# Query-key products of a sparse attention layer: summed over features on TensorE by accumulated transposes, with biases added by transposes

## The chip, the cores and the metric

The kernel runs on one core of a Trainium2 chip. The metric is the device time of the whole kernel in microseconds (us). A core has TensorE (PE, matrix products; its weight loads are listed as PEld), VectorE (DVE), ScalarE (ACT), GpSimd (POOL), and SyncE (SP), which here only starts transfers. The engines run side by side, each works through its own instructions in order, and they wait for each other by semaphores. Products of PE land in PSUM, eight banks of 128 partitions by 512 fp32 numbers.

## What is computed

Two graph layers over 8 batches of 2048 nodes with 256 features. A node has few neighbours (the adjacency is sparse and symmetric, with the diagonal). Layer 0 is attention with 4 heads of 64 features, whose softmax runs over chunks of 256 nodes, with absent edges at a score of -10:

```python
q = (x @ Wq.T + bq).reshape(B, N, H, Dh).transpose(0, 2, 1, 3)
k = (x @ Wk.T + bk)...
v = (x @ Wv.T + bv)...
scores = jnp.einsum('bhnd,bhjcd->bhnjc', q, kc) / jnp.sqrt(Dh)
scores = jnp.clip(scores, -10.0, 10.0)
scores = jnp.where(mask == 0, -10.0, scores)
attn = jax.nn.softmax(scores, axis=-1)          # over the 256 nodes of a chunk
ctx = jnp.einsum('bhnjc,bhjcd->bhnd', attn, vc)
out = ctx @ Wo.T + bo + x
out = layernorm(out) * gamma + beta
x = _layernorm(x + out)
# ... layer 1: a second graph attention, whose scores are s_src + s_dst of
# Wh = x @ W, then softmax over neighbours, sum of Wh, elu
x = _layernorm(x + layer1)
```

## The kernel before

The kernel builds a list of neighbours for each node (24 places), sorts the nodes by their number of neighbours, and cuts them into 16 tiles of 128 nodes. Tile t has room for `CAPS[t]` neighbours. Two batches make a group, so there are 4 groups of layer 0, 64 iterations, each for one group and tile. For layer 1 two groups are taken together, 32 iterations. A table of keys and values (`kv_d`), made by `tables`, lies in HBM; GpSimd gathers from it one row of 4 KB per node and neighbour slot, two slots to a unit, into a ring of 12 units.

```python
G = 2; UNIT = 2; RING = 12       # batches per group, neighbours per unit, units
CAPS = (24, 14, 13, 12, 11, 11, 10, 10, 9, 9, 8, 8, 7, 7, 6, 5)
# GF = 512: features of a group; GH = 8: heads of a group; KC = 2; D = 64; NCH = 8
```

A PSUM bank is taken by tag; the tags `tk` (2 banks), `tf` (1), `acc` (3) and `mf` (2) make up the eight banks:

```python
    def bank(tag, bufs=2):

        return ps.tile([P, 512], F32, tag=tag, name=tag, bufs=bufs)
    def transposed(t, tag, bufs):

        pt = bank(tag, bufs).rearrange("p (c r) -> p c r", r=P)
        for c in range(G * KC):
            nc.tensor.transpose(pt[:, c, :], t[:, c * P:(c + 1) * P], ident)
        return pt
```

The tables of one tile: transposes of x, keys and values of each batch, queries of both. The bias is added by a product of a row of ones with the bias row:

```python
    def tables(g, t):
        if t == 0:
            vsum[g] = small.tile([P, G * KC, NT], F32, tag="xs", name="xs")
        qx = xts.pop((g, t))
        pt = transposed(qx[:, GF:], "tk", 2)
        xT = work.tile([P, G * KC, P], F32, tag="xT", name="xT")
        for c in range(G * KC):
            nc.scalar.activation(xT[:, c, :], pt[:, c, :], AF.Copy, accum_out=vsum[g][:, c, t:t + 1])
        kvs = work.tile([P, 2 * GF], F32, tag="kvs", name="kvs", bufs=1)
        view = kvs.rearrange("p (m b f) -> p b m f", m=2, b=G)
        for b in range(G):
            pm = bank("tk")
            for kc in range(KC):
                nc.tensor.matmul(pm, xT[:, b * KC + kc, :], wkv[:, kc, :], start=(kc == 0), stop=False, skip_group_check=True)
            nc.tensor.matmul(pm[:, 0:F], ones1, bk_r, start=False, stop=True, skip_group_check=True)
            nc.scalar.copy(view[:, b], pm.rearrange("p (m f) -> p m f", m=2))
        nc.sync.dma_start(kv_d[g][t * P:(t + 1) * P, :], kvs)
        q = bank("tk")
        for b in range(G):
            qb = q[:, b * F:(b + 1) * F]
            for kc in range(KC):
                nc.tensor.matmul(qb, xT[:, b * KC + kc, :], wq[:, kc, :], start=(b == 0 and kc == 0), stop=False,
                                 skip_group_check=True)
            nc.tensor.matmul(qb, ones1, bq_r, start=False, stop=True, skip_group_check=True)
        nc.scalar.copy(qx[:, 0:GF], q)
        nc.sync.dma_start(qx_d[g][t * P:(t + 1) * P, :], qx)
    # ... (sums of v per chunk after the last tile)
```

The weighting of gathered rows and their sum, by transposes that accumulate in PSUM:

```python
    def weighted(part, al, s0, n):

        e = part.shape[2] // D
        pv = part.rearrange("p s (e d) -> p s e d", d=D)
        av = al[:, :, s0:s0 + n].rearrange("p e s -> p s e").unsqueeze(3).to_broadcast([P, n, e, D])
        nc.vector.tensor_tensor(pv, pv, av, op=ALU.mult)

    def summed(acc, part, first, last):

        n = part.shape[1]
        for k in range(n):
            for c in range(G * KC):
                nc.tensor.matmul(acc[:, c, :], part[:, k, c * P:(c + 1) * P], ident, is_transpose=True,
                                 start=first and k == 0 and c == 0, stop=last and k == n - 1, skip_group_check=True)
```

Layer 0. `scores0` multiplies the gathered keys by the query in place, and reduces over the 64 features of each head; both run on VectorE:

```python
    def fetch0(g, t):
        qx = work.tile([P, 2 * GF], F32, tag="qx", name="qx", bufs=3)
        nc.gpsimd.indirect_dma_start(out=qx, out_offset=None, in_=qx_d[g],
                                     in_offset=bass.IndirectOffsetOnAxis(ap=node[:, t:t + 1], axis=0))
        got0[g, t] = qx, gather(2 * GF, kv_d[g], t)

    def scores0(g, t):
        S = CAPS[t]
        qx, units = got0[g, t][:2]
        sc = small.tile([P, GH, S], F32, tag="sc", name="sc")
        for u, s0, n in units:
            part = u[:, :, 0:GF]
            nc.vector.tensor_tensor(part, part, qx[:, 0:GF].unsqueeze(1).to_broadcast([P, n, GF]), op=ALU.mult)
            nc.vector.tensor_reduce(sc[:, :, s0:s0 + n].rearrange("p e s -> p s e"),
                                    part.rearrange("p s (e d) -> p s e d", d=D), axis=AX.X, op=ALU.add)
        st0[g, t] = sc

    def softmax0(g, t):
        S = CAPS[t]
        sc = st0.pop((g, t))
        nc.vector.tensor_scalar(sc, sc, -10.0, 10.0, op0=ALU.max, op1=ALU.min)
        e = small.tile([P, GH, S], F32, tag="e", name="e", bufs=1)
        nc.scalar.activation(e, sc, AF.Exp)
        nc.vector.scalar_tensor_tensor(e, e, -EMIN, valid[:, t, 0:S].unsqueeze(1).to_broadcast([P, GH, S]),
                                       op0=ALU.add, op1=ALU.mult)
        # ... sums of e by chunk into z, its reciprocal, the weights al
        pz = bank("tf", 1)[0:H * NCH, 0:G * P].rearrange("p (b r) -> p b r", b=G)
        for b in range(G):
            nc.tensor.transpose(pz[:, b, :], z[:, b * H:(b + 1) * H, :].rearrange("p h c -> p (h c)"), ident)
        zT = small.tile([H * NCH, G, P], F32, tag="zT", name="zT")
        nc.scalar.copy(zT, pz)
        st0[g, t] = al, zT

    def context0(g, t):
        S = CAPS[t]
        al, zT = st0.pop((g, t))
        units = got0[g, t][1]
        acc = bank("acc", 3).rearrange("p (c r) -> p c r", r=P)
        for b in range(G):
            for kc in range(KC):
                nc.tensor.matmul(acc[:, b * KC + kc, :], vsum[g][:, b, kc * P:(kc + 1) * P], zT[:, b, :],
                                 start=(b == 0 and kc == 0), stop=False, skip_group_check=True)
        for u, s0, n in units:
            weighted(u[:, :, GF:2 * GF], al, s0, n)
            summed(acc, u[:, :, GF:2 * GF], False, s0 + n == S)
        cT = work.tile([P, G * KC, P], F32, tag="cT", name="cT", bufs=1)
        nc.scalar.copy(cT, acc)
        st0[g, t] = cT
    def finish0(g, t):
        cT = st0.pop((g, t))
        qx, _, xb = got0.pop((g, t))
        po = bank("mf").rearrange("p (b f) -> p b f", b=G)
        for b in range(G):
            for kc in range(KC):
                nc.tensor.matmul(po[:, b, :], cT[:, b * KC + kc, :], wo[:, kc, :], start=(b == 0 and kc == 0),
                                 stop=False, skip_group_check=True)
            nc.tensor.matmul(po[:, b, :], ones1, bo_r, start=False, stop=True, skip_group_check=True)
        o = work.tile([P, G, F], F32, tag="o", name="o")
        nc.vector.tensor_tensor(o, po, qx[:, GF:].rearrange("p (b f) -> p b f", b=G), op=ALU.add)
        # ... moments, layer norms (VectorE, with Ln and Exp on ScalarE)
        normalized(o, o, G)
        nc.sync.dma_start(x1_d[g // 2][t * P:(t + 1) * P, g % 2, :].rearrange("p (b f) -> p b f", b=G), o)

        pt = transposed(o.rearrange("p b f -> p (b f)"), "tf", 1)
        xT = work.tile([P, G * KC, P], F32, tag="x1T", name="x1T", bufs=1)
        nc.scalar.copy(xT, pt)
        wh = work.tile([P, WW], F32, tag="whs", name="whs")
        for b in range(G):
            pw = bank("mf")
            for kc in range(KC):
                nc.tensor.matmul(pw[:, 0:F + 2 * H], xT[:, b * KC + kc, :], wa[:, kc, :], start=(kc == 0), stop=(kc == KC - 1))
            nc.scalar.copy(wh[:, b * F:(b + 1) * F], pw[:, 0:F])
            nc.scalar.copy(sd[g // 2 % 2][:, t, g % 2, b * H:(b + 1) * H], pw[:, F:F + H])
            nc.scalar.copy(wh[:, GF + b * H:GF + (b + 1) * H], pw[:, F + H:F + 2 * H])
        # ... scatter of wh by GpSimd
```

Layer 1's `context1` uses two `acc` banks per iteration (one per group of the pair), and its `finish1` turns the sums back through `mf`, one bank for each of the two:

```python
        for k, hT in enumerate(hTs):
            ph = bank("mf")
            for c in range(G * KC):
                nc.tensor.transpose(ph[:, c * P:(c + 1) * P], hT[:, c, :], ident)

            nc.scalar.activation(y[:, k], ph, AF.Exp)
            nc.vector.scalar_tensor_tensor(xr[:, k], ph, 0.0, xr[:, k], op0=ALU.max, op1=ALU.add)
            # ...
```

The sequence: groups 0 and 1 of layer 0 first, then groups 2 and 3 with the first half of layer 1 between them, then the rest of layer 1. Instructions are ordered for each engine when the program is built, so that those of neighbouring steps are interleaved:

```python
    seq = [(0, i) for i in range(2 * NT)]
    for t in range(NT):
        seq += [(0, 2 * NT + 2 * t), (0, 2 * NT + 2 * t + 1), (1, t)]
    seq += [(1, NT + t) for t in range(NT)]
# ...
    for k, (layer, i) in enumerate(seq):
        g, t = i // NT, i % NT
        if layer == 0:
            shift0(g, t)
        scatters()
        # ... fetch of the next step
        if layer == 0:
            scores0(g, t)
            if i:
                finish0((i - 1) // NT, (i - 1) % NT)
            if g + 1 < NG:
                if i + NT + 1 < NG * NT:
                    load_x((i + NT + 1) // NT, (i + 1) % NT)
                tables(g + 1, t)
            if k + 1 < len(seq) and seq[k + 1] == (0, (g + 1) * NT):
                fetch[0](seq[k + 1][1])
            softmax0(g, t)
            context0(g, t)
        else:
            softmax1(g, t)
            if i:
                finish1((i - 1) // NT, (i - 1) % NT)
            context1(g, t)
```

## Time and profile before

| | before |
|---|---|
| time, median of 3 runs | 3197.0 us (3189.07 to 3202.07) |
| span of the profiled execution | 3192.1 us |
| instructions | 31721 |
| TensorE clock granted, mean | 0.771 |
| HBM read and written | 604.31 MB and 117.96 MB |

The span is the time from the first to the last instruction. A group of the profile is named by its line in the kernel, the engine and the operation, with the tile written and the tiles read; behind the bar stand its busy time, the mean duration of one instruction in ns, and the idle time of the engine just before, with what ended it. An fp32 product of the program stands as two records on PE and a transpose as one: the 128 products with `bk_r` are 256 records, the 256 transposes of `qxs` 256. Records of PE overlap each other, so that a duration is longer than the time from one start to the next. The line numbers are those of the kernel before.

### The profile page before, as it was taken

How to read it: one execution, taken by the hardware profiler on the slowest of the kernel's cores; microseconds unless marked ns; L12 is line 12 of the kernel's file. 1: busy time of each engine (PE TensorE's matmuls, PEld its weight loads, DVE VectorE, ACT ScalarE, POOL GpSimd, SP SyncE). 2: the span in 40 equal slices, each digit the busy share in tenths (PEclk: the TensorE clock that was granted, in tenths of full speed). 3: DMA queues.
4: the chain of work that ended last, by engine and by line, in shares of the span. 5: the costliest groups of instructions: out<-in, count | busy, mean ns of one | idle time of the engine just before them, and what ended most of it. 6: DMA issues, size and time to landing. Idle time of an engine off the chain costs nothing. (4 is left out here: it accounts for less than half of the span.)

```text
span 3192.1 us, 31721 instructions
## 1 busy us (share of the span) xinstructions
PE 1991.3 (62%) x9554; PEld 1373.5 (43%) x9554; DVE 2512.5 (79%) x4912; ACT 695.1 (22%) x2140; POOL 1746.2 (55%) x1364
## 2 busy tenths in 40 slices
PE   7988955599988886554455555453554554346553
PEld 3444534355555554333344444342433443235452
DVE  5925789886688888777989988889999887368785
ACT  3632211133322222111011111111111212112222
POOL 0053656534276445436667666557776543488873
PEclk8999977789997888666777776676776667677876
DMA  5645765566477756426657666636676653367771
GB/s 194 231 143 215 287 230 189 199 212 218 171 264 260 257 203 227 151 94 203 228 189 264 223 229 215 208 114 240 220 243 227 230 180 110 131 213 274 269 250 66
DMA packets 219466, 660.18 MB, mean 207 GB/s; under 512 B 43688, under 2 KB 61867, under 8 KB 217239
## 3 DMA queue, kind: packets, MB, share of 16 engines
q0 software_dynamic: 162688, 521.98, 48.2%
q1 hardware_dynamic: 52880, 126.11, 10.7%
q10 hardware_dynamic: 3718, 9.97, 0.9%
q8 instruction: 79, 1.29, 0.2%
q14 instruction: 101, 0.82, 0.1%
HBM read 604.31 MB, written 117.96 MB: 226 GB/s over the span
## 5 line engine op out<-in xcount | busy, mean ns | idle before, releaser
L385 POOL DMA_INDIRECT u<-kv_d,idx x656 | 812.8, 1239 | 323.4 <-issue 143.0
L404 PE MATMUL acc<-ident,u 128*128 128x128 f32 x5248 | 692.0, 293 | 247.5 <-DVE u L397 236.2
L404 PEld LDWEIGHTS acc<-ident,u 128*128 128x128 f32 x5248 | 640.1, 152 | 297.5 <-DVE u L397 271.7
L426 DVE TENSOR_TENSOR u<-u,qx 128x1024 f32<-128x1024 f32 (+1 forms) x344 | 401.6, 1177 | 164.8 <-DMA u<-kv_d,idx 131.9
L274 PE MATMUL tf<-ident,o 128*128 128x128 f32 x256 | 68.9, 410 | 712.4 <-ACT o L377 712.3
L385 POOL DMA_INDIRECT u<-wh_d,idx x328 | 420.4, 1282 | 129.0 <-issue 70.7
L515 POOL DMA_INDIRECT wh_d<-whs,node x64 | 144.5, 2258 | 593.4 <-ACT zT L458 542.6
L427 DVE TENSOR_REDUCE sc<-u 128x16 f32<-128x1024 f32 (+1 forms) x344 | 393.2, 1158 | 0.8
L397 DVE TENSOR_TENSOR u<-u,e 128x1024 f32<-128x1024 f32 (+1 forms) x344 | 387.6, 1164 | 0.2
L397 DVE TENSOR_TENSOR u<-u,al 128x1024 f32<-128x1024 f32 (+1 forms) x344 | 386.0, 1175 | 0.6
L274 PEld LDWEIGHTS tf<-ident,o 128*128 128x128 f32 x256 | 36.8, 192 | 750.9 <-ACT o L377 742.1
L296 PE MATMUL tk<-wkv,xT 128*128 128x512 f32 x512 | 312.6, 736 | 46.8 <-ACT xT L290 37.0
L511 PE MATMUL mf<-wa,x1T 128*128 128x264 f32 x512 | 215.2, 590 | 31.1 <-ACT x1T L506 31.1
L589 POOL DMA_INDIRECT out_dram<-y,nodeb x128 | 162.6, 1270 | 89.3 <-ACT y L377 54.2
L511 PEld LDWEIGHTS mf<-wa,x1T 128*128 128x128 f32 x512 | 144.0, 294 | 90.1 <-ACT x1T L506 53.6
L352 ACT ACTIVATE y<-mv,eps 128x2 f32<-128x2 f32 (+1 forms) x160 | 47.2, 295 | 575.2 <-DVE mv L367 575.2
L296 PEld LDWEIGHTS tk<-wkv,xT 128*128 128x128 f32 x512 | 100.7, 222 | 157.2 <-issue 84.8
L490 PE MATMUL mf<-wo,cT 128*128 128x256 f32 x512 | 143.9, 401 | 22.4 <-ACT cT L474 22.3
L304 PE MATMUL tk<-wq,xT 128*128 128x256 f32 x512 | 151.4, 415 | 8.7 <-ACT kvs L298 8.6
L531 DVE TENSOR_TENSOR z<-u,sd 128x16 f32<-128x16 f32 (+1 forms) x344 | 44.9, 185 | 112.2 <-DMA u<-wh_d,idx 112.2
L298 ACT COPY kvs<-tk 128x512 f32<-128x512 f32 x128 | 74.8, 585 | 262.9 <-PE tk L297 191.2
L480 POOL TENSOR_TENSOR xb<-qx,beta_r 128x512 f32<-128x512 f32 x64 | 82.5, 1291 | 82.9 <-DVE o L500 81.9
(144 smaller groups left out, 2909.6 us busy)
## 6 DMA issues: line engine op xcount, KB each, us to landing
kv_d<-kvs SPq DMA_DIRECT2D x64, 512.0 KB, 3.3
qx_d<-qxs SPq DMA_DIRECT2D x64, 512.0 KB, 5.0
qxs<-in_x_dram SPq DMA_DIRECT2D x64, 256.0 KB, 3.2
x_d<-o SPq DMA_DIRECT2D x64, 256.0 KB, 2.0
xr<-x_d SPq DMA_DIRECT2D x32, 512.0 KB, 6.7
u<-kv_d,idx POOLq DMA_INDIRECT x656, 5.9
at<-in_adj_dram SPq DMA_DIRECT2D x8, 1024.0 KB, 8.1
at<-in_adj_dram ACTq DMA_DIRECT2D x8, 1024.0 KB, 6.5
```

The source lines that it names most:

```text
L274: nc.tensor.transpose(pt[:, c, :], t[:, c * P:(c + 1) * P], ident)
L296: nc.tensor.matmul(pm, xT[:, b * KC + kc, :], wkv[:, kc, :], start=(kc == 0), stop=False, skip_group_check=True)
L304: nc.tensor.matmul(qb, xT[:, b * KC + kc, :], wq[:, kc, :], start=(b == 0 and kc == 0), stop=False, skip_group_check=True)
L385: nc.gpsimd.indirect_dma_start(out=u[:, k, 0:width], out_offset=None, in_=table, in_offset=bass.IndirectOffsetOnAxis(ap=idx[:, t, s0 + k:s ...
L397: nc.vector.tensor_tensor(pv, pv, av, op=ALU.mult)
L404: nc.tensor.matmul(acc[:, c, :], part[:, k, c * P:(c + 1) * P], ident, is_transpose=True, start=first and k == 0 and c == 0, stop=last and ...
L426: nc.vector.tensor_tensor(part, part, qx[:, 0:GF].unsqueeze(1).to_broadcast([P, n, GF]), op=ALU.mult)
L427: nc.vector.tensor_reduce(sc[:, :, s0:s0 + n].rearrange("p e s -> p s e"), part.rearrange("p s (e d) -> p s e d", d=D), axis=AX.X, op=ALU.add)
L490: nc.tensor.matmul(po[:, b, :], cT[:, b * KC + kc, :], wo[:, kc, :], start=(b == 0 and kc == 0), stop=False, skip_group_check=True)
L511: nc.tensor.matmul(pw[:, 0:F + 2 * H], xT[:, b * KC + kc, :], wa[:, kc, :], start=(kc == 0), stop=(kc == KC - 1))
L515: late.append(lambda: nc.gpsimd.indirect_dma_start(out=wh_v[g // 2][g % 2 * NT + t], out_offset=bass.IndirectOffsetOnAxis(ap=node2[:, g % ...
L589: nc.gpsimd.indirect_dma_start(out=out_v[t * B + b], out_offset=bass.IndirectOffsetOnAxis(ap=nodeb[:, t, b:b + 1], axis=0), in_=yv[:, b - ...
```

## The change

The sum over features moves to TensorE. The features of a head are cut into 8 parts (`NJ`) of 8 features (`DP`), and the tables of queries and keys are stored part by part, so that in each part the 8 heads of a group lie side by side (64 numbers). VectorE still multiplies, now into a tile of its own, `prod`. Eight transposes, one per part, accumulate into one place of a PSUM bank `pr`, which sums over the parts; ScalarE copies the sums of up to four units to SBUF (`prT`), and a small product with a 0/1 matrix `sel` adds the 8 features that are left, and puts the scores, with nodes back on partitions, into a bank `tf`. The reductions of VectorE fall away. The biases are held as columns (`biasT`), and are added by transposes of a column that is broadcast to 128x128, in place of the products with a row of ones.

The banks are dealt out anew: `tk` 2, `tf` 2, `acc` 2, `mf` 1, `pr` 1. To save room the softmax of the widest tile is done in two halves, and `xb` overwrites the query part of `qx`. The core of the diff (the constants and the preparation of weights and biases are cut, and so are further lines that only change the number of banks, `bank("mf")` to `bank("mf", 1)` and `bank("acc", 3)` to `bank("acc")`):

```diff
 D = 64
+DP = 8
+NJ = D // DP
 ...
+    def add_bias(dst, k):
+
+        for c in range(KC):
+            nc.tensor.matmul(dst[:, c * P:(c + 1) * P], biasT[:, k, c:c + 1].to_broadcast([P, P]), ident,
+                             is_transpose=True, start=False, stop=c == KC - 1, skip_group_check=True)
 ...
-        view = kvs.rearrange("p (m b f) -> p b m f", m=2, b=G)
+        vk = kvs[:, 0:GF].rearrange("p (j b f) -> p b j f", b=G, j=NJ)
         for b in range(G):
             pm = bank("tk")
             for kc in range(KC):
                 nc.tensor.matmul(pm, xT[:, b * KC + kc, :], wkv[:, kc, :], start=(kc == 0), stop=False, skip_group_check=True)
-            nc.tensor.matmul(pm[:, 0:F], ones1, bk_r, start=False, stop=True, skip_group_check=True)
-            nc.scalar.copy(view[:, b], pm.rearrange("p (m f) -> p m f", m=2))
+            add_bias(pm[:, 0:F], 1)
+            nc.scalar.copy(vk[:, b], pm[:, 0:F].rearrange("p (j f) -> p j f", j=NJ))
+            nc.scalar.copy(kvs[:, GF + b * F:GF + (b + 1) * F], pm[:, F:])
         nc.sync.dma_start(kv_d[g][t * P:(t + 1) * P, :], kvs)
         q = bank("tk")
         for b in range(G):
@@ -303,8 +336,9 @@
             for kc in range(KC):
                 nc.tensor.matmul(qb, xT[:, b * KC + kc, :], wq[:, kc, :], start=(b == 0 and kc == 0), stop=False,
                                  skip_group_check=True)
-            nc.tensor.matmul(qb, ones1, bq_r, start=False, stop=True, skip_group_check=True)
-        nc.scalar.copy(qx[:, 0:GF], q)
+            add_bias(qb, 0)
+        nc.scalar.copy(qx[:, 0:GF].rearrange("p (j b f) -> p b j f", b=G, j=NJ),
+                       q.rearrange("p (b j f) -> p b j f", b=G, j=NJ))
 ...
     def scores0(g, t):
         S = CAPS[t]
         qx, units = got0[g, t][:2]
-        sc = small.tile([P, GH, S], F32, tag="sc", name="sc")
-        for u, s0, n in units:
-            part = u[:, :, 0:GF]
-            nc.vector.tensor_tensor(part, part, qx[:, 0:GF].unsqueeze(1).to_broadcast([P, n, GF]), op=ALU.mult)
-            nc.vector.tensor_reduce(sc[:, :, s0:s0 + n].rearrange("p e s -> p s e"),
-                                    part.rearrange("p s (e d) -> p s e d", d=D), axis=AX.X, op=ALU.add)
-        st0[g, t] = sc
+        ps_sc = bank("tf")[:, 0:GH * S].rearrange("p (s e) -> p s e", e=GH)
+        W8 = GH * DP
+        for i in range(0, len(units), 4):
+            some = units[i:i + 4]
+            pr = bank("pr", 1).rearrange("p (k r) -> p k r", r=P)
+            for k, (u, s0, n) in enumerate(some):
+                prod = work.tile([P, NJ, UNIT * W8], F32, tag="prod", name="prod")
+                nc.vector.tensor_tensor(prod[:, :, 0:n * W8].rearrange("p j (s w) -> p s j w", w=W8),
+                                        u[:, :, 0:GF].rearrange("p s (j w) -> p s j w", w=W8),
+                                        qx[:, 0:GF].rearrange("p (j w) -> p j w", w=W8).unsqueeze(1)
+                                        .to_broadcast([P, n, NJ, W8]), op=ALU.mult)
+                for j in range(NJ):
+                    nc.tensor.matmul(pr[0:n * W8, k, :], prod[:, j, 0:n * W8], ident, is_transpose=True,
+                                     start=(j == 0), stop=(j == NJ - 1), skip_group_check=True)
+            m = len(some)
+            prT = work.tile([P, 4, P], F32, tag="prT", name="prT", bufs=1)
+            full = m - 1 if some[-1][2] < UNIT else m
+            if full:
+                nc.scalar.copy(prT[:, 0:full, :], pr[:, 0:full, :])
+            if full < m:
+                nc.scalar.copy(prT[0:W8, full, :], pr[0:W8, full, :])
+            for k, (u, s0, n) in enumerate(some):
+                nc.tensor.matmul(ps_sc[:, s0:s0 + n, :], prT[0:n * W8, k, :], sel[0:n * W8, 0:n * GH],
+                                 start=(s0 == 0), stop=(s0 + n == S), skip_group_check=True)
+        st0[g, t] = ps_sc
 
     def softmax0(g, t):
         S = CAPS[t]
-        sc = st0.pop((g, t))
-        nc.vector.tensor_scalar(sc, sc, -10.0, 10.0, op0=ALU.max, op1=ALU.min)
+        sc = small.tile([P, GH, S], F32, tag="sc", name="sc", bufs=1)
+        nc.vector.tensor_scalar(sc, st0.pop((g, t)).rearrange("p s e -> p e s"), -10.0, 10.0, op0=ALU.max, op1=ALU.min)
 ... # the softmax, in halves for the widest tile
-        pz = bank("tf", 1)[0:H * NCH, 0:G * P].rearrange("p (b r) -> p b r", b=G)
+        pz = bank("tf")[0:H * NCH, 0:G * P].rearrange("p (b r) -> p b r", b=G)
 ...
     def shift0(g, t):
         qx, units = got0[g, t]
-        xb = work.tile([P, G, F], F32, tag="xb", name="xb")
+        xb = qx[:, 0:GF].rearrange("p (b f) -> p b f", b=G)
         nc.gpsimd.tensor_tensor(xb, qx[:, GF:].rearrange("p (b f) -> p b f", b=G),
                                 beta_r.unsqueeze(1).to_broadcast([P, G, F]), op=ALU.add)
         got0[g, t] = qx, units, xb
     def finish0(g, t):
         cT = st0.pop((g, t))
         qx, _, xb = got0.pop((g, t))
-        po = bank("mf").rearrange("p (b f) -> p b f", b=G)
+        po = bank("mf", 1).rearrange("p (b f) -> p b f", b=G)
         for b in range(G):
             for kc in range(KC):
                 nc.tensor.matmul(po[:, b, :], cT[:, b * KC + kc, :], wo[:, kc, :], start=(b == 0 and kc == 0),
                                  stop=False, skip_group_check=True)
-            nc.tensor.matmul(po[:, b, :], ones1, bo_r, start=False, stop=True, skip_group_check=True)
+            add_bias(po[:, b, :], 2)
 ...
-        if layer == 0:
-            shift0(g, t)
+        if seq[k - 1][0] == 0 and k:
+            shift0(seq[k - 1][1] // NT, seq[k - 1][1] % NT)
         scatters()
```

## The prediction

> **What bounds the kernel now.** I read the busy shares first, then split the span into stages, then read the waits and one stretch of the timeline. The page gives only an average:
>
> ```profile
> PE 1991.3 (62%) x9554; PEld 1373.5 (43%) x9554; DVE 2512.5 (79%) x4912; ACT 695.1 (22%) x2140; POOL 1746.2 (55%) x1364
> ```
>
> VectorE (DVE) is the busiest, but no engine is full, so the stages must be told apart. The clip of the scores (L434) runs once per layer-0 iteration; its start times mark the stages: first at 280 us, then groups 0 and 1 until 1415, group 2 until 2127, group 3 until about 2690, and after that only layer 1. The windows view of these stretches (columns: stretch, its length, busy time of each engine with instruction counts, granted TensorE clock, DMA share, GB/s):
>
> ```profile
> 0.00:210.00 210.00, 177.60 (x513) 84.55 (x514) 136.82 (x495) 100.09 (x244) 22.87 (x50) 0.92 0.55 192
> 210.00:280.00 70.00, 60.30 (x172) 27.58 (x170) 32.49 (x28) 17.41 (x66) 53.27 (x40) 0.89 0.68 248
> 280.00:866.00 586.00, 453.99 (x1866) 279.71 (x1866) 439.32 (x717) 138.91 (x509) 280.69 (x211) 0.84 0.60 210
> 866.00:1415.00 549.00, 417.31 (x1715) 257.60 (x1713) 437.28 (x730) 123.78 (x446) 275.57 (x213) 0.81 0.61 212
> 1415.00:2127.00 712.00, 359.32 (x2096) 288.14 (x2096) 620.90 (x1139) 113.05 (x339) 451.05 (x346) 0.71 0.62 207
> 2127.00:2690.00 563.00, 281.57 (x1583) 224.08 (x1584) 512.12 (x976) 103.00 (x307) 347.50 (x268) 0.70 0.62 210
> 2690.00:3192.00 502.00, 241.22 (x1615) 211.88 (x1613) 333.55 (x834) 98.88 (x230) 315.21 (x239) 0.74 0.55 192
> ```
>
> Stage A (0 to 280) is the edge lists plus the first tables: PE is busy 85% of it. Stage B (280 to 1415) is layer 0 of groups 0 and 1 with the tables of the later groups: PE 77%, DVE 77%, alternating. Stage C (1415 to 2690) is layer 0 of groups 2 and 3 with the first half of layer 1: DVE 1133 of 1275 us, 89%, PE only 50%. Stage D is the rest of layer 1.
>
> That B has two limits shows in narrower windows. From 500 to 600 DVE is full, from 800 to 900 PE is:
>
> ```profile
> 500.00:600.00 100.00, 47.92 (x226) 35.86 (x226) 92.39 (x156) 15.14 (x51) 67.37 (x48) 0.68 0.65 220
> 800.00:900.00 100.00, 93.12 (x396) 56.64 (x397) 66.37 (x96) 27.38 (x99) 39.00 (x32) 0.93 0.52 177
> ```
>
> So an exchange of VectorE work for TensorE work pays fully in C, and in B only as far as PE has room.
>
> **What the Trainium skill says.** "VectorE: DVE Perf Modes", the perf-mode tier table, puts fp32 tensor_tensor and every tensor_reduce at one element per cycle, and its rules for kernel authors call the reduction the slowest operation and advise restructuring. The trace agrees that multiply and reduction cost the same (rows below: 1228 and 1207 ns for 1024 elements), so dropping the reductions halves the score work there. "TensorE: Matmul & The Clock Gate", Part 1, says that PE runs at half clock until it has been busy for a while; the spacing of transposes here is about 0.11 us warm, and gaps near 0.21 occur where PE had idled, so the trace agrees. Part 4 of that page says that transposes do not warm the clock. I doubt it here: stage D, whose PE work is almost all transposes, was granted 0.74, no lower than C at 0.71. "PSUM — Partial Sum Buffer", the four PSUM rules, names the eight banks: the new bank for accumulated products must be taken from other tags, and it is, from `acc` and `mf`.
>
> **The change, part by part.** The groups concerned:
>
> ```profile
> L427 DVE TENSOR_REDUCE sc<-u 128x16 f32<-128x1024 f32 x312 | 372.6, 1207 | 0.7
> L426 DVE TENSOR_TENSOR u<-u,qx 128x1024 f32<-128x1024 f32 x312 | 380.8, 1228 | 164.8 <-DMA u<-kv_d,idx 131.9 <-DMA qx<-qx_d,node 24.5 <-issue 4.3
> L404 PE MATMUL acc<-ident,u 128*128 128x128 f32 x5248 | 692.0, 293 | 247.5 <-DVE u L397 236.2 <-DVE r L355 7.2
> L297 PE MATMUL tk<-bk_r,ones 1*128 1x256 f32 x256 | 96.9, 460 | 0.0
> L306 PE MATMUL tk<-bq_r,ones 1*128 1x256 f32 x256 | 91.2, 436 | 0.0
> ```
>
> *Removed from DVE:* 344 reductions, 393.2 us by the page (312 at 1207 ns and 32 half ones). Half of them lie in B, half in C: 197 us each. The multiplications stay. They write to a second buffer in runs of 64 elements; I count the same 1.2 us.
>
> *PE prices.* Durations of records overlap, so I take start-to-start times from the timeline at 760 to 800 us, where PE has no gaps:
>
> ```profile
> 785.61 3.28 PE L404 MATMUL acc<-ident,u 128*128 128x128 f32 x28
> 788.82 0.69 PE L297 MATMUL tk<-bk_r,ones 1*128 1x256 f32 x2
> 789.45 0.70 PE L304 MATMUL tk<-wq,xT 128*128 128x256 f32 x2
> ```
>
> 28 transposes take 788.82 - 785.61 = 3.21 us, 0.115 each; a bias product (one fp32 product, two records) takes 789.45 - 788.82 = 0.63. From the eight records of L468 just before (784.53 to 785.61) a small fp32 product costs 2 x 0.135 = 0.27.
>
> *Added on PE:* per unit of two neighbours 8 transposes and one product with `sel`: 8 x 0.115 + 0.27 = 1.19 us; times 344 units = 409 us, 205 in B and 205 in C.
>
> *Bias:* two transposes for one product, 0.63 - 0.23 = 0.40 saved, 384 times (4 per table, 2 per finish) = 154 us. By the starts of the copy that ends each table (L307), 25 of the 64 tables run in A and 39 in B: 40 us off A, 62 off B; the 32 finishes each in B and C give 26 and 26.
>
> *Moved:* ScalarE gets one copy of up to 128x512 per four units (0.59 us, as L474) and two half copies in place of one in the tables; at 22% busy it has room. `mf` drops from two banks to one and `acc` from three to two; `tf` goes from one to two. VectorE's clip now waits for a chain: last multiply, 8 transposes (0.9), copy (0.6), small products (up to 4 x 0.27), with semaphores some 3 us, where before it followed the last reduction at once.
>
> *Sum by stage.* A: 40 us off PE, which is 85% busy, but 16 tables' worth (26 us) of it lies in the first 210 us, where PE is the steady load; I take -20. B: PE goes from 871 to 871 + 205 - 62 - 26 = 988 us, DVE from 877 to 680. PE becomes the bound. At the best share seen (93%) that is 1062 us against 1135; a busier PE should also be granted more than the present 0.82 of its clock, while one-bank waits cost. I take 1045: -90. C: DVE goes from 1133 to 936; at the present 89% that is 1052. Of the 3 us chain in 32 iterations (96 us) I let half be hidden by other work that the built order places there, and add 20 for the single `mf` bank: 48 + 20 + 1052 = 1120, against 1275: -155, and I keep -140 because GpSimd's gathers (799 us busy in C) must now fit in a shorter stage. D has no score work and loses only banks: +10. Sum: -20 - 90 - 140 + 10 = -240, so 3197 - 240 = 2957; I say 2955.
>
> **The rivals.** *PE takes over and eats the gain in B.* For: 988 us of PE in a 1135 us stage, and transposes that come in packets of eight behind VectorE may run cold at 0.21. Against: the built order spreads the tables over B (about 1.2 per iteration instead of bunches), and the bias saves 88 us there. If B gains nothing: 3045. *The score chain stalls VectorE.* One `pr` bank and one `prT` buffer let one group of four units go at a time, and PE runs in order behind context transposes. For: `prod` has two buffers, so VectorE can be only two units ahead. Against: other vector work stands between. If all 96 us of C's chain is exposed and 1 us more per group is lost: C about 1230, total near 3060. *Gathers become the bound.* For: VectorE already waits for them:
>
> ```profile
> DVE u L426 <- DMA u<-kv_d,idx: 131.9, 38, 30.9
> DVE z L531 <- DMA u<-wh_d,idx: 112.2, 43, 8.4
> ```
>
> Against: the mean DMA share is 0.62 in C and GpSimd is 63% busy there; a stage 12% shorter makes that some 71%. It would cost up to 60 us: 3010. *All overlap is better than I think*: B at 970 and C at 1060 would give about 2820.
>
> **Range and chances.** One rival at full strength leaves 3010 to 3060, two together about 3110; the good case is near 2830. So 2830 to 3110, with 2955 near the middle. Slower by over 2% would need the 393 us of VectorE to be wholly replaced by new waits in both stages: 0.07. Within 2% (3133 to 3261) needs most of it: 0.10. Faster by over 2%: 0.83.
>
> **What would show it.** Right: VectorE total near 2120 us with no L427, its multiplication still near 1.2 us; PE total up by some 200 us rather than 400; PE busy over 85% in B; C shorter by 100 to 180 us, D unchanged within 20. Wrong: multiplications well above 1.3 us (the strided write costs); a VectorE wait at the clip for `tf` of over 150 us in sum; PE transposes of `prod` spaced at 0.2 us; stage D longer by over 30 us (the banks mattered). The prediction as a whole fails if PE or the chain stalls lengthen B beyond 1135 us.

## The result and the profile after

The changed kernel takes 3109.2 us (median of 4 runs, 3103.7 to 3120.8) against 3198.8 us for the kernel before, with a fourth run of it: a ratio of 0.973, interval 0.9691 to 0.9768. It is faster, by 90 us, where 242 were predicted. The busy times of the page:

```profile
PE 2198.2 (71%) x13006; PEld 1749.5 (56%) x13006; DVE 2184.7 (70%) x4592; ACT 756.8 (24%) x2404; POOL 1673.6 (54%) x1367
```

VectorE lost 328 us of the 393 predicted, and PE gained 207, near the prediction. The time did not follow them. The stages are cut again at the starts of the clip of the scores (L434, now L486). First B and C of the kernel before, then B, C and D of the changed kernel in the windows view (columns as in the prediction: stretch, length, busy PE, PEld, DVE, ACT, POOL, granted clock, DMA share, GB/s):

```profile
280.00:1415.00 1135.00, 871.30 (x3579) 537.31 (x3578) 876.61 (x1446) 262.70 (x955) 556.26 (x423) 0.82 0.61 211
1415.00:2669.00 1254.00, 633.97 (x3649) 507.61 (x3650) 1115.76 (x2056) 209.54 (x628) 791.18 (x608) 0.71 0.62 210
```

```profile
280.00:1320.00 1040.00, 880.23 (x5243) 681.30 (x5242) 708.88 (x1289) 286.34 (x1077) 515.77 (x423) 0.92 0.66 228
1320.00:2599.00 1279.00, 859.25 (x5319) 718.40 (x5320) 983.68 (x1952) 244.75 (x716) 766.03 (x615) 0.77 0.62 209
2599.00:3102.00 503.00, 248.36 (x1574) 219.16 (x1573) 339.94 (x844) 99.14 (x223) 317.52 (x238) 0.70 0.54 192
```

From here on C ends at the start of the last clip (2669 us in the kernel before, not 2690 as in the prediction's estimate), so that it is cut alike in all kernels. Each length is that of one profiled execution. In one measurement executions of the kernel before took from 3190 to 3235 us, so a difference of some 20 us between two stages says little. The last clip also does not stand at the same place among the other work in all kernels: three finishes of layer 0 follow it in the kernel before, two in the changed kernel. C and D are therefore told together where that matters.

| stage | before, us | after, us | difference | predicted |
|---|---|---|---|---|
| A | 280 | 280 | 0 | -20 |
| B | 1136 | 1040 | -96 | -90 |
| C | 1254 | 1279 | +25 | -140 |
| D | 523 | 504 | -19 | +10 |

So one number needs an explanation above all: C has 132 us less VectorE work than before (1116 to 984) and is not shorter; C and D together are 6 us longer. The groups of the new score work (busy, mean ns of one; then the idle time before and what ended it):

```profile
L464 DVE TENSOR_TENSOR prod<-u,qx 128x1024 f32<-128x1024 f32 x312 | 379.6, 1223 | 304.7 <-DMA u<-kv_d,idx 183.2 <-PE pr L469 73.4 <-DMA qx<-qx_d,node 23.0
L469 PE MATMUL pr<-ident,prod 128*128 128x128 f32 x2496 | 391.3, 305 | 283.0 <-DVE prod L464 252.3 <-DVE r L391 16.7 <-DVE nm L409 11.4
```

The multiplication kept its 1.22 us in the new layout. Where VectorE stands now, over the whole span (columns: what waits, for what, us in total, times, longest):

```profile
DVE sc L486 <- PE tf L479: 206.7, 35, 13.1
DVE prod L464 <- DMA u<-kv_d,idx: 183.2, 65, 31.3
DVE z L586 <- DMA u<-wh_d,idx: 144.1, 52, 12.1
...
DVE prod L464 <- PE pr L469: 74.4, 33, 8.6
```

The first is the new wait of the clip for the score chain (62.3 us of it in C), and so is the last, for a free `prod`. The other two are the old waits for gathers, grown from 131.9 and 112.2 us. In C alone PE, too, stands in a place that the change does not touch, the transposes of the normalized output `o` in finish0 (L300):

```profile
PE pr L469 <- DVE prod L464: 183.4, 61, 15.6
PE tf L300 <- ACT o L411: 171.0, 17, 17.9
```

In C of the kernel before it stood there (then L274) for longer:

```profile
PE tf L274 <- ACT o L377: 530.9, 30, 31.3
```

One of the waits of the changed kernel on PE's part of the timeline (start, duration; in brackets the idle time before):

```profile
1593.25 1.18 PE L300 MATMUL tf<-ident,o 128*128 128x128 f32 x4 [16.23 <-ACT o L411]
1594.22 0.64 PE L511 MATMUL tf<-ident,z 128*32 128x128 f32 x2
1595.11 2.13 PE L566 MATMUL mf<-wa,x1T 128*128 128x264 f32 x4 [0.25 <-ACT x1T L561]
1597.16 1.65 PE L523 MATMUL acc<-zT,vs 32*128 32x128 f32 x6
1598.74 2.13 PE L566 MATMUL mf<-wa,x1T 128*128 128x264 f32 x4
1600.80 0.79 PE L523 MATMUL acc<-zT,vs 32*128 32x128 f32 x2
1601.52 4.73 PE L438 MATMUL acc<-ident,u 128*128 128x128 f32 x25
```

VectorE multiplied a unit by its weights at 1586.48 us (1.19 us), so that unit was ready at 1587.7. PE took it only at 1601.5, since its queue is in order. L300 and the product L566 of the tile before stood ahead of it, and with them the transposes of `z` and the opening products of its own tile (L511, L523). Of the 13.8 us of delay, 5.6 are PE's wait at L300, and the rest is the work listed. Units are freed by L438, so the next gathers came late as well.

### The profile page after: what moved, and what is told of

Read it like the earlier page. It is cut to its first block, busy times and chain, and to the rows that moved or that the text cites. A ratio compares the mean times of both kernels' runs of the same rounds, so it can differ in the third digit from the quotient of the medians.

```text
span 3102.7 us, 38815 instructions
## 1 busy us (share of the span) xinstructions
PE 2198.2 (71%) x13006; PEld 1749.5 (56%) x13006; DVE 2184.7 (70%) x4592; ACT 756.8 (24%) x2404; POOL 1673.6 (54%) x1367
## 5 line engine op out<-in xcount | busy, mean ns | idle before, releaser
L438 PE MATMUL acc<-ident,u 128*128 128x128 f32 x5248 | 694.1, 292 | 103.1 <-DVE u L431 94.9
L438 PEld LDWEIGHTS acc<-ident,u 128*128 128x128 f32 x5248 | 637.9, 152 | 155.0 <-DVE u L431 137.2
L469 PE MATMUL pr<-ident,prod 128*128 128x128 f32 (+1 forms) x2752 | 428.3, 304 | 293.8 <-DVE prod L464 261.7
L464 DVE TENSOR_TENSOR prod<-u,qx 128x1024 f32<-128x1024 f32 (+1 forms) x344 | 400.8, 1173 | 305.9 <-DMA u<-kv_d,idx 183.2
L469 PEld LDWEIGHTS pr<-ident,prod 128*128 128x128 f32 (+1 forms) x2752 | 347.9, 154 | 372.5 <-DVE prod L464 314.0
L570 POOL DMA_INDIRECT wh_d<-whs,node x64 | 75.6, 1181 | 551.8 <-ACT whs L569 518.5
L328 PE MATMUL tk<-wkv,xT 128*128 128x512 f32 x512 | 271.1, 641 | 27.5 <-ACT xT L322 27.5
L300 PE MATMUL tf<-ident,o 128*128 128x128 f32 x256 | 66.7, 378 | 204.4 <-ACT o L411 203.9
L566 PE MATMUL mf<-wa,x1T 128*128 128x264 f32 x512 | 193.7, 514 | 8.7 <-ACT x1T L561 6.1
L300 PEld LDWEIGHTS tf<-ident,o 128*128 128x128 f32 x256 | 37.4, 185 | 228.9 <-ACT o L411 224.1
L450 POOL DMA_INDIRECT qx<-qx_d,node x64 | 88.4, 1381 | 135.8 <-issue 123.6
L486 DVE TENSOR_SCALAR sc<-tf 128x192 f32<-128x192 f32 (+7 forms) x64 | 15.3, 239 | 206.7 <-PE tf L479 206.7
L634 PE MATMUL mf<-ident,hT 128*128 128x128 f32 x256 | 50.6, 330 | 151.4 <-DVE xr L637 148.2
L566 PEld LDWEIGHTS mf<-wa,x1T 128*128 128x128 f32 x512 | 114.8, 247 | 50.6 <-ACT x1T L561 18.2
```

The source lines that it names most:

```text
L464: nc.vector.tensor_tensor(prod[:, :, 0:n * W8].rearrange("p j (s w) -> p s j w", w=W8), u[:, :, 0:GF].rearrange("p s (j w) -> p s j w", w=W8),
L469: nc.tensor.matmul(pr[0:n * W8, k, :], prod[:, j, 0:n * W8], ident, is_transpose=True, start=(j == 0), stop=(j == NJ - 1), skip_group_chec ...
L570: late.append(lambda: nc.gpsimd.indirect_dma_start(out=wh_v[g // 2][g % 2 * NT + t], out_offset=bass.IndirectOffsetOnAxis(ap=node2[:, g % ...
```

## The experiments

The theories. *Hidden limit*: C was not bound by VectorE's work, busy as it was, but by the order of PE's queue and by the ring of 12 gathered units; the change relieves an engine that only filled waits. *Score chain*: VectorE was the bound, and the new chain took back what the change gave. *Banks*: the `mf` and `acc` banks that were given up cost it. *Gathers*: GpSimd's work per gather, or the transfers' bytes. A ratio below is to the kernel before, with its interval.

| run | B | C | D | ratio |
|---|---|---|---|---|
| before | 1136 | 1254 | 523 | |
| after | 1040 | 1279 | 504 | 0.973 (0.9691 to 0.9768) |
| reductions cut, e1 | 1095 | 1231 | 522 | 0.968 (0.9596 to 0.9765) |
| banks only, e2 | 1105 | 1341 | 522 | 1.005 (1.0023 to 1.0077) |
| bias only, e3 | 1098 | 1282 | 514 | 0.986 (0.9795 to 0.9922) |
| scores only, e4 | 1188 | 1360 | 506 | 1.045 (1.0368 to 1.0523) |
| after, tail moved, e5 | 936 | 1229 | 507 | 0.930 (0.9234 to 0.9356) |
| before, tail moved, e6 | 979 | 1274 | 505 | 0.946 (0.9399 to 0.9529) |
| after, ring 14, e16 | 1005 | 1271 | 502 | 0.962 (0.9563 to 0.9679) |
| before, ring 14, e14 | 1107 | 1215 | 524 | 0.972 (0.966 to 0.9777) |
| after, tail and ring, e12 | 893 | 1158 | 497 | 0.891 (0.8875 to 0.8952) |
| before, tail and ring, e17 | 994 | 1181 | 508 | 0.929 (0.9209 to 0.9374) |
| e17, reductions cut, e18 | 898 | 1116 | 514 | 0.875 (0.8666 to 0.8829) |

**Reductions cut.** The kernel before, its reduction reading one element of 64: the sum over features is left out, and nothing is put in its place.

```
- part.rearrange("p s (e d) -> p s e d", d=D), axis=AX.X
+ part.rearrange("p s (e d) -> p s e d", d=D)[:, :, :, 0:1], axis=AX.X
```

> The kernel before, with each reduction of a score cut to one element of 64 (the sum over features is left out; 344 reductions of about 1.15 us become some 0.1 us), nothing added on TensorE. It measures what taking the work off VectorE can bring at most. Theory 'order' (in groups 2 and 3 the time is set by a loop of waits: the transposes of the finish stand in TensorE's queue ahead of the context transposes, units stay held, gathers stop, VectorE waits): groups 0 and 1 gain 50 to 100 us, groups 2 and 3 gain under 60 of the 190 us taken off VectorE, total about 3060 to 3120. Rival 'chain' (the gain in groups 2 and 3 was there and was eaten by the new wait for multiply, transposes, copy and small products): groups 2 and 3 gain 120 us or more, total under 2980.

Its stages B and C in the windows view:

```profile
274.00:1369.00 1095.00, 876.17 (x3609) 540.30 (x3608) 725.97 (x1452) 265.77 (x968) 507.01 (x424) 0.84 0.64 221
1369.00:2600.00 1231.00, 643.48 (x3652) 516.63 (x3653) 984.79 (x2054) 210.59 (x628) 788.49 (x607) 0.70 0.64 214
```

VectorE lost 131 us in C and C lost 23; in B it lost 151 for 41. No chain, no added transposes, no banks are in this kernel, so the predicted gain of C was missing before anything was added. That is the premise of the prediction, not its costs. The figure is rough: the stages of the two executions differ by 70 us in sum, while the ratio makes the whole gain 102 us (75 to 129), so the 23 may be too low by some 30. By the prediction's busy share it was to be 131 / 0.89 = 147. In VectorE's waits in C, that for a unit with keys is 90.9 us here, 28.9 in the kernel before: the freed time became waiting for gathers.

**Banks only.** The kernel before with the changed kernel's banks: two `acc`, one `mf`, two `tf`.

```
- acc = bank("acc", 3)      + acc = bank("acc")
- po = bank("mf")           + po = bank("mf", 1)
- pz = bank("tf", 1)        + pz = bank("tf")
```

> The kernel before with the changed kernel's PSUM banks (acc 2 in place of 3, mf 1 in place of 2, tf 2 in place of 1; pr is not used), all else as before. Theory 'banks' (the single mf bank and the two acc banks ate the gain of groups 2 and 3): slower by 60 us or more, over 3255, most of it in groups 2 and 3. Theory 'order': within 30 us of before.

The whole is 0.5% longer, some 16 us. The build moved 8 of the 64 tables from B into C, so the stages are told together: in single executions B and C make 2446 us against 2390. *Banks* is a small cost at most, not 165 us.

**Bias only, scores only.** The first is the kernel before with `add_bias`; the second is the changed kernel with its biases as products with a row again.

```
- nc.tensor.matmul(pm[:, 0:F], ones1, bk_r, start=False, stop=True)
+ add_bias(pm[:, 0:F], 1)          # bias only; likewise for q and for finish0

- nc.tensor.matmul(dst[:, c * P:(c + 1) * P], biasT[:, k, c:c + 1].to_broadcast([P, P]), ident, is_transpose=True, ...)
+ nc.tensor.matmul(dst, ident[0:1, 0:1].to_broadcast([1, P]), bias_r[:, k, :], start=False, stop=True)   # scores only
```

> The kernel before with the biases added by transposes, scores and banks unchanged. By the prediction's prices 154 us of TensorE time fall away, 62 of them in groups 0 and 1, where TensorE is the limit part of the time: those groups shorter by 30 to 60 us, groups 2 and 3 by under 15, total 3120 to 3165. If TensorE's order and not its load counts: under 20 us in all.

> The changed kernel with the biases added by a product of a row of ones again (384 products of 0.63 us in place of 768 transposes of 0.115): scores on TensorE alone. If the two parts add up, its gain is that of the changed kernel (90 us) less that of the bias part: 3130 to 3190; if TensorE is the limit in groups 0 and 1 in the changed kernel, these groups get longer by 50 us or more against the changed kernel. Groups 2 and 3 within 30 us of the changed kernel.

Stage B of bias only, then of scores only:

```profile
272.00:1370.00 1098.00, 700.01 (x3458) 513.57 (x3459) 876.66 (x1445) 249.03 (x915) 575.82 (x423) 0.80 0.61 213
```

```profile
299.00:1487.00 1188.00, 1064.29 (x5275) 727.26 (x5275) 704.63 (x1293) 291.35 (x1096) 510.08 (x423) 0.88 0.58 201
```

The score part adds 193 us of PE work in B (871 to 1064; predicted 205), the bias part takes 171 off (to 700; predicted 88). Three tables went from B to C in that build; over the whole span PE fell by 206 us, where 154 were predicted. Alone, the score part makes PE 90% busy in B and the kernel 4.5% slower, and there PE is the bound: the bias part then takes 184 us of PE work off B (1064 to 880) and shortens it by 148. So the rival "PE takes over" is real, and the bias part is what wards it off. The two parts do not add: -1.4% and +4.5% alone, -2.7% together. C of scores only is 81 us longer than in the changed kernel, where 30 at most were expected. About 60 of the bias products lie in C, some 36 us at the price below, so most of the 81 is not explained.

Why the bias saves more is in the timeline. The kernel before, output product and bias:

```profile
1700.48 1.13 PE L490 MATMUL mf<-wo,cT 128*128 128x256 f32 x4 [0.46 <-ACT cT L474]
1701.54 0.69 PE L492 MATMUL mf<-bo_r,ones 1*128 1x256 f32 x2
1702.17 1.13 PE L490 MATMUL mf<-wo,cT 128*128 128x256 f32 x4
```

The four records ahead of the bias take 1.06 us and the bias 0.63. In the changed kernel the same product:

```profile
1669.30 1.03 PE L545 MATMUL mf<-wo,cT 128*128 128x256 f32 x4
1670.17 0.38 PE L306 MATMUL mf<-ident,biasT 128*128 128x128 f32 x2
```

Now the four take 0.87, and the two transposes 0.22 by the spacing of other pairs. The product with one row had also lengthened the spacing of its neighbours: 309 ns from the record before it to its own start and 320 between the first two of the next four, against 216 for the others. The saving is (1.06 + 0.63) - (0.87 + 0.22) = 0.60 us, not 0.40.

**Tail moved.** finish0 is cut where its transposes begin; they, the product with `wa` and the copies are called after the context of the next tile. Once in the changed kernel, once in the kernel before.

```
+     st0[g, t] = o
+ def tail0(g, t):
+     o = st0.pop((g, t))
      pt = transposed(o.rearrange("p b f -> p (b f)"), "tf", 2)
...
      context0(g, t)
+     if i:
+         tail0((i - 1) // NT, (i - 1) % NT)
```

> The changed kernel with the second half of the finish (transposes of the normalized rows, product with wa, copies, scatter) called after the context of the same step in place of before its softmax; same work. Theory 'order': TensorE no longer stands at these transposes while weighted units wait for it, so groups 2 and 3 (1279 us) shrink by 80 us or more, total under 3030. Rival 'chain' (the score chain is what holds groups 2 and 3): within 30 us of the changed kernel, 3080 to 3140. A third, that GpSimd's queue holds it, since the scatter now comes later still: slower than the changed kernel.

> The same move of the finish's second half in the kernel before. Theory 'order': there VectorE with its reductions fills more of the waits (89% busy in groups 2 and 3), so the move brings less than in the changed kernel: 3120 to 3180. If it brings as much as there (80 us or more), the order is a limit of its own, apart from the change.

PE's wait in C at these transposes fell from 171.0 us to:

```profile
PE tf L300 <- ACT o L411: 10.6, 2, 10.4
```

B lost 104 us and C 50 against the changed kernel, less in C than the 80 that the order was to be worth there; 7 tables went from B into C in the build, so a part of the 104 belongs to C. In the kernel before, B and C together lost 136 (14 tables went from B to C, so the stages are not told apart). The order is thus a limit of its own, in both kernels; it does not explain why the change gained so little.

**Where the scatter lies.** GpSimd waits for `whs` to scatter `wh_d`, 518.5 us in sum in the changed kernel, with gathers queued behind. Three kernels: the scatter issued a step later; the scatter replaced by a plain store from another queue, which leaves the rows in the sorted order; and that with the tail moved.

```
- late.append(lambda: nc.gpsimd.indirect_dma_start(out=wh_v[...], out_offset=..., in_=wh, in_offset=None))
+ late.append(lambda: nc.sync.dma_start(wh_v[...][rows], wh))
```

> The changed kernel with each scatter (of wh and of the output) put into GpSimd's queue one step later, behind one more step's gathers. Theory 'GpSimd' (gathers are held up behind a scatter that waits for the finish, 230 us in groups 2 and 3): groups 2 and 3 shrink by 60 us or more. Theory 'order' (the ring is full at that time, since TensorE has not yet released the units): under 30 us.

> The changed kernel with the scatter of wh replaced by a plain store of the same bytes from SyncE's queue (the rows are left in sorted order, so layer 1 works on other rows; as many bytes and gathers as before). GpSimd no longer waits for the finish. Theory 'scatter' (the 231 us that GpSimd waits at the scatter in groups 2 and 3 hold back the gathers that VectorE then waits for): groups 2 and 3 shrink by 60 us or more. Theory 'ring' (the 12 units hold two steps, and gathers can start only once TensorE has released units): the wait moves to the ring, groups 2 and 3 shrink by under 30 us.

> The same plain store in the kernel with the finish's second half moved behind the context (the run with the tail moved), where GpSimd waits only 57 us at the scatter in groups 2 and 3 but 150 us for units. Theory 'scatter': 20 to 50 us off groups 2 and 3. Theory 'ring': within 15 us of that run.

The first says nothing: the scheduler put the scatter nearly where it was, and its wait in C went from 230.6 to 192.7 us only (0.974, 0.9672 to 0.9814). The second removes the wait, and C goes from 1279 to 1273 (0.977, 0.9732 to 0.9815). GpSimd then waits as long over the span, in another place:

```profile
POOL u L419 <- PE acc L438: 659.9, 117, 20.1
```

That is a wait for a free unit of the ring. On the kernel with the moved tail the plain store gives B -29 and C +2 (0.920, 0.9149 to 0.9257). The scatter is not what sets C.

**Half rows.** The changed kernel with layer 0's gathers cut to half rows (the values are left out; the keys are summed in their place).

```
- got0[g, t] = qx, gather(2 * GF, kv_d[g], t)
+ got0[g, t] = qx, gather(GF, kv_d[g].rearrange("n (h w) -> (n h) w", h=2), t)
```

> The changed kernel with gathered key and value rows of half the length (2 KB in place of 4; the values are left out and the keys are weighted in their place), as many gathers as before; the rows of layer 1 as they were. About a third of the bytes of groups 2 and 3 and half of those of groups 0 and 1 fall away. Theory 'transfers' (VectorE's 167 us of waits for gathers in groups 2 and 3 are bandwidth or landing time): groups 2 and 3 shrink by 80 us or more. Theory 'order': under 30 us.

B 1016, C 1356 (0.989, 0.9833 to 0.9955): C is 77 us longer, though it moved about a quarter fewer bytes (144 GB/s over 1356 us against 209 over 1279; the gathers of layer 1 are as before). So this run gives no sign that bandwidth sets C. Why C is longer is not known. There are as many gathers as before, so GpSimd's work per gather is not tested by it, nor by any other run.

**The ring.** A ring of 14 units needs room: `hT`, `xr` and `y` share buffers of the tables, `valid` is held as bf16, and the tables are made somewhat faster than one per iteration. With these edits the ring was run at 12 and at 14, on three bases.

```
- RING = 12
+ RING = 14
```

> Control for the next run: the kernel with the tail moved, with room made in SBUF (the tables' tiles are reused by layer 1 after the last table, all tables called three per two steps in groups 0 and 1; softmax in halves for more tiles), ring of 12 units as before. Groups 0 to 3 together within 40 us of the kernel with the tail moved (2165 us from first clip to last).

> The control with a ring of 14 units in place of 12, nothing else. Theory 'ring' (after the tail is moved, what holds groups 2 and 3 is the loop release of units, gather, landing, scores, context): groups 2 and 3 shrink by 40 us or more against the control, and VectorE's waits for gathers (183 us there in the kernel with the tail moved) fall by half. If the ring is not the limit: within 15 us of the control.

> The kernel before with the room made in SBUF (tables called three per two steps in groups 0 and 1, their tiles reused by layer 1), ring of 12: a control, 3120 to 3230.

> The same with a ring of 14. Theory 'ring': VectorE is 89% busy in groups 2 and 3 here, so little is left to gain: groups 2 and 3 shrink by 20 to 60 us against the control. If the ring were a limit apart from the change, they shrink as much as the changed kernel's.

> The changed kernel (finish not moved) with the same room, ring of 12: control, 3060 to 3140. Against the control of before, groups 2 and 3 gain under 40 us, as without the room.

> The same with a ring of 14. Theory 'ring': groups 2 and 3 shrink by 60 us or more against its control, so that the change is worth 40 us or more in more of these groups than at 12 units. Theory 'order' (TensorE's queue standing at the finish is the limit without regard to the ring): under 30 us.

The edits alone do nothing on the kernels as they were (1.000, 0.9971 to 1.0029 on before; 0.977, 0.9711 to 0.9833 on after); with the tail moved they give some 29 us (2964.6 to 2935.5). Two units more then give: with the tail moved, 2935.5 to 2837.8 us (C 1218 to 1158); on the unmoved changed kernel, 3123.9 to 3069.6 (C 1280 to 1271); on the kernel before, 3193.4 to 3104.5 (C 1265 to 1215). VectorE's waits, tail moved, with a ring of 12:

```profile
DVE prod L464 <- DMA u<-kv_d,idx: 188.2, 66, 31.2
DVE z L590 <- DMA u<-wh_d,idx: 138.8, 48, 10.1
```

and with 14:

```profile
DVE prod L464 <- PE pr L469: 127.2, 68, 10.2
DVE prod L464 <- DMA u<-kv_d,idx: 120.1, 46, 33.6
DVE z L590 <- DMA u<-wh_d,idx: 105.1, 42, 8.8
...
DVE sc L486 <- PE tf L479: 31.6, 29, 3.5
```

The waits for gathers fell by a third and a quarter, not by half. In C of the changed kernel one move helps little without the other: moving the tail alone gives 50 us, the ring alone 9, both 121 (in the whole time some 140, 50 and 260). One expectation fell: the change was to gain more on a ring of 14. In C it did the opposite, +56 us there (1215 to 1271) against +15 on a ring of 12 (1265 to 1280). So the ring alone does not uncover the gain.

**Both limits moved in the kernel before.** This is the test that the whole argument needs: if both limits are moved first, is the predicted gain there?

```
  # the kernel before, with tail0 and RING = 14 as above; then with the reductions cut as in the first experiment
```

> The kernel before with both limits moved: finish0's second half behind the context of the next tile, and a ring of 14 units. Against it stands the changed kernel with the same two moves: 2838 us, stage B 893, stage C 1158. Theory 'uncovered': the predicted worth of the change was there, but hidden behind TensorE's queue and the ring. Then VectorE, with 1116 us of work in C, sets C here: C stays at 1210 us or more, the whole at 2990 us or more, so the change is worth 5% or more on this base. Theory 'never there': VectorE's reductions fill waits whatever the other limits are. Then both moves add up as on their own (the move 3028 us, the ring about 80 less): about 2945 us or below, and the change is worth under 4% on this base.

> The same kernel with the reductions cut to a copy of one element of each 64 (the sum is left out) and nothing added to TensorE. On the unmoved kernel this gave 41 us in B and 23 in C. Theory 'uncovered': with the other two limits moved, C falls by 80 us or more against the kernel beside it, out of 131 us taken off VectorE there. Theory 'never there': by 30 us or less in C. In B, where TensorE has about 870 us of work, the gain is bounded by that: no less than 900 us is expected by either.

Stage C of the kernel before with both moves, and the same with the reductions cut:

```profile
1273.00:2454.00 1181.00, 682.00 (x3694) 534.16 (x3692) 1115.05 (x2091) 219.25 (x645) 842.24 (x611) 0.73 0.67 224
```

```profile
1168.00:2284.00 1116.00, 690.93 (x3715) 544.91 (x3714) 966.80 (x2081) 219.15 (x644) 839.69 (x614) 0.74 0.72 240
```

VectorE is now 94% busy in C, and taking 148 us off it gives 65, in place of 23 for 131. In B, 96 for 164 in place of 41 for 151. In the whole time the relief is worth 168 us (2963.4 to 2795.4), in place of 102. The 2963 us of the first kernel and the 65 us of the second lie between what the two theories expected: a part of the gain had been hidden behind the two limits, but at the busy share of 94% the 148 us were to bring 157.

PE's stand had not gone from C of the kernel before, either. It had moved to the transposes of `z` in the softmax:

```profile
PE tf L457 <- DVE r L357: 162.7, 11, 31.9
```

With its other entries PE waits there for some 350 us in C, in place of 24 at `z` and 531 at `o`. In the changed kernel with both moves it waits 54 us there.

## Why the prediction was right or wrong

**The step that failed** is "C: DVE goes from 1133 to 936; at the present 89% that is 1052". It divides VectorE's work by its busy share and so takes VectorE for the engine that sets C. The relief of VectorE and the cost of what is added can be told apart on both bases, in C:

| | as it was | tail moved, ring 14 |
|---|---|---|
| VectorE relieved, nothing added | 1254 to 1231: -23 | 1181 to 1116: -65 |
| the rest of the change added | 1231 to 1279: +48 | 1116 to 1158: +42 |
| together | +25 | -23 |

With D counted in, the rows are -24, +30 and +6 as it was, and -59, +26 and -34 with both moves. The added part was put too high rather than too low: 68 us in C (48 for the chain and 20 for the bank) and 10 in D. The relief was put at 1275 - 1052 = 223 us and is 23 (by the whole time up to some 50). Two things are in that. VectorE's busy time fell by 132 us, not 197: the 160 reductions of C took 184 us and are gone, other groups grew by some 30 (`z` alone from 31.6 to 42.4), and durations overlap at their ends, so that the sum of all of them in C fell by 155 us but the busy time by 132. And each microsecond taken off was worth about a sixth. The reading of the waits is that VectorE at 89% was waiting its turn in a cycle: unit gathered, multiplied, transposed by PE in queue order, freed, gathered again. I followed the releases back through C of the kernel before, from the last clip: VectorE's work is about 590 us of the 1254 on that path, and of the 184 us of reductions only 57 lie on it. In the kernel before with both moves the same path has 68, where the cut gave 65. This agrees with the gains better than the busy share does. The path is my working from the trace's releases; the cuts of the reductions are what shows the small worth.

"Perfetto Trace Analysis", § Identifying the Most-Contended Engine, counsels to take the engine of the highest occupancy and to optimize it first. In C that is VectorE by a long way (1116 us against 791 for the next), and cutting it gave 23 us where moving one block of PE's program and adding two units gave 73 (1254 to 1181); the measurement decides. The same page, § Optimization Strategy, says that a gap which repeats can mean that SBUF or PSUM has no room for the next tile. The runs with a ring of 14 agree: 98 us for two more units.

**A** (-20): nothing came in sum. The tables there lost PE work (178 to 150 us in the first 210 us). But the scores of the first tile lie in A, which the prediction left out: in single executions A is 299 us with the scores alone, 272 with the biases alone, and 280 in both kernels. The prediction also misread where the tables lie: 22 end in A and 42 in B, not 25 and 39, which moves some 5 us of saving from A to B.

**B** (-90): -96, near in sum by luck, since the terms are others. PE was to go to 988 us and bound the stage; it went from 871 to 880. The bias part saves half as much again per product, and the granted clock rose from 0.82 to 0.92, which shortens the same work; the two are not told apart. With PE 85% busy at 1040 us, the step's "best share seen (93%)" was not reached; with both moves it was (831 of 893). In the scores-only kernel, where PE had 1064 us, the step's picture holds: 90% busy and the stage 1188.

**C** (-140): see above. The rival "the score chain stalls VectorE" is a part of the +48, and the clip's wait for `tf` came to 206.7 us in sum, over the 150 that the prediction gave as a sign of being wrong. With both limits moved it is 31.6, so most of it was PE's queue and not the chain's own length. In exchange VectorE's wait for a free `prod` rose from 74.4 to 127.2, and no run gave `prod` a third buffer or `pr` a second bank.

**D** (+10): -19, with the border to C at another place. With the banks alone D stays at 522 us, so they did not matter there.

The signs named ahead: multiplication near 1.2 us, right; VectorE total near 2120, measured 2185; PE up by some 200, right (207); transposes of `prod` at 0.2 us, mostly did not come (from start to start 84% of them stand 0.11 us apart in B and 59% in C, where a quarter stand at 0.2); C shorter by 100 to 180 us, wrong.

What stays open: with both limits moved, 148 us of VectorE still buy only 65 in C. What holds the rest is not settled; its waits there are again for gathers (156.1 us over the span for a unit with keys, 71.3 with the reductions in). PE's order still has its share there, as the wait at `z` shows, and GpSimd is 75% busy in C (839.7 of 1116 us) with a number of gathers that no run varied. Half rows did not help in the unmoved changed kernel, and were not tried here.

With the two moves the changed kernel takes 2837.8 us, 0.891 of the kernel before and faster than either kernel; against the kernel before with the same moves (2963.4) the change itself is worth 125 us, 101 of it in B.

## What to carry to other kernels

An engine that is busy 89% of a stage is its bound only if shortening its work shortens the stage; before an exchange of engines is priced, cut the work out without replacement and time that. Where units of a ring pass several in-order engines, look for the instruction in each queue that waits for something unrelated to the unit behind it: moving one such block, and two more units, brought more than the whole exchange. Price each part of a change by itself, as the parts may need each other: the score part alone was a loss.

## What the runs showed of the hardware

- An fp32 product of one row cost more than itself: 0.63 us for 1x256, and a record of the 128-row product on either side of it took 309 and 320 ns from start to start instead of 216. Two transposes of a broadcast column add the same bias for 0.22 us.
- Transposes did raise PE's granted clock. "TensorE: Matmul & The Clock Gate", Part 4, says that full clock does not engage for them; the trace shows otherwise. After 2780 us PE runs nothing but transposes in the kernel before (L404 and L579), and the clock changes between full and half: from 2925.7 us, where PE is 78% busy, it is 1.0 for 13.7 us and the transposes stand 109 ns apart, and in the 10.2 us before that, at 27%, it is 0.5 and they stand 213 ns apart. In B the clock likewise rose with the busy share: 0.82 at 77% (before), 0.92 at 85% (after), and 0.91 at 89% in the kernel with both moves and the reductions cut, which has none of the added transposes.
- Half the bytes per gathered row of layer 0 did not shorten C: 1356 us against 1279.
